# Two group-normed 5x5 convolutions: another buffer for one row tile, row additions earlier in the queue, a group mean later

## The chip, the cores and the metric

The kernel runs on one core of a Trainium2 chip. The metric is the device time of one execution in microseconds, taken as the median of several runs. The core has a matrix engine (TensorE, called PE in the profile, with its weight loads as PEld), a vector engine (VectorE, DVE), a scalar engine (ScalarE, ACT), a general engine (GpSimd, POOL) and a queue engine (SyncE, SP). Each engine works through its own list of instructions in the order in which the program gave them to it, and waits where an instruction needs something that is not ready. Transfers are issued here from SP's queue (image rows, statistics pieces, weights, results) and from POOL's queue (the copies and additions described below).

## The reference

There are eight images of 32 channels and 252 x 252 pixels in float32. Two layers follow each other, and each does the same thing with its own weights:

```
def layer(x, weight):
    g = groupnorm(x, 16 groups of 2 channels, eps 1e-5)   # mean and variance over 2*252*252 values
    return x + conv5x5(g, weight)                         # reflect-padded at the borders
x = layer(layer(x, L0_conv_weight), L1_conv_weight)
```

The reference computes the convolution by FFT; the kernel computes it directly. The normalisation is folded into the weights (a scale per channel) and a bias, and the residual addition of x is folded in as further weight entries.

## The kernel before, in words

**Tiling.** In the code the two layers are `l = 0` and `l = 1`, and below they are named by this index. An image is cut into 8 chunks of 16 row pairs (`c = 0..7`), so there are 8 x 2 x 8 = 128 units `(b, l, c)`. A unit is a Winograd-like convolution over rows: row differences and sums of the input are formed (points 0 to 5), multiplied on PE with transformed weights `u`, and combined into four output rows. PE works through the points in the order 2, 4, 1, 3 and later 0 and 5; each is three products (`product`, L671 to L682, `h = 0, 1, 2`), and each float32 product stands in the trace as two matmul records.

**Row differences v.** Points 4, 3, 1 and 0/5 need the tile `v`, the differences or sums of rows two apart. For `l = 0` DVE computes `v` (`row_pairs`, L556, the subtraction is L561). For `l = 1` transfers compute it (`row_sums`, L544): one call with `add = False` copies the unit's rows from `y` into `v` (POOL's queue, L551), and a later call with `add = True` adds the rows two further down onto it (L553, and L554 for the last two rows from the next chunk). The additions must wait until the copy has landed. The pool of `v` has one buffer per name: `row_pairs` uses the name `v`, and `row_sums` uses `va`, except for the last ten units, where it alternates between the two. The last reader of a `v` is `points05` (L603) on DVE. `point4` (L590, DVE) is the first to read the finished `v`.

**Order.** Nothing is scheduled by a compiler. Every piece of work is entered in a table with a due time (`at(t, fn, ...)`), the table is sorted by time, and the instructions are issued in that order. The times are not clock times: they only set the order on each engine. Units have slots starting at `begin(i)`, and the list `order` interleaves `l = 0` of image b+1 with `l = 1` of image b. Around the first image it runs

```
... (0,0,7) (1,0,0) (1,0,1) (0,1,0) (0,1,1) (1,0,2) (0,1,2) (1,0,3) ...
i:    7       8       9       10      11      12      13      14
```

so that (0,1,0) and (0,1,1) are the only two units with `l = 1` that follow directly on each other before the end of the list. With the times of the code, `begin(7)` is 107.1, `begin(8)` 122.4, `begin(9)` 132.6, `begin(10)` 147.9 and `begin(11)` 168.3.

**Statistics and weights.** When an image's last chunk of a layer is reached, `finish_stats` enters six steps: `moments` (DVE, L328 to L336), `group_mean` (PE, L342 and L344: tiny matmuls with averaging matrices into the spare columns of bank `m24[0]`), `deviations` (DVE, L351 to L357), `group_var` (PE, L363), `variance` (DVE L369 and ACT L371) and `inverse` (DVE, to L383). Then the weights are scaled by ACT for the points 2 and 4, then 1 and 3, then 0 and 5 (`scale_points`, L511), and POOL adds the residual's entries to each group (`add_residual`, L479, four instructions per group). PE's products of a point need its scaled weights with the residual added. I call the three groups of `add_residual` the first, second and third residuals.

**What stands near each other on POOL's list.** POOL has, besides `row_sums` and `add_residual`, the reflected borders of the input tiles `xs` (`borders`, L148 to L154), which wait for input loads issued by SP (L143).

Of the kernel before, what the change touches and what calls it, by code (L numbers as in the profile page):

```python
# [56 lines left out]
def tile_conv_preact_x2(ctx: ExitStack, tc: tile.TileContext, x: bass.AP, w0: bass.AP, w1: bass.AP, out: bass.AP):  # L57
    nc = tc.nc
    B, C, H, W = x.shape
# [5 lines left out]
    NCH = 8  # L65
# [26 lines left out]
    def at(t: float, fn, *args, **kw):  # L92
        table.append((t, len(table), fn, args, kw))
# [67 lines left out]
    def once(b: int, c: int) -> bool:  # L161

        return c < (NCH - 1, 3)[b] if b < 2 else False

    def parts(b: int, c: int):

        if once(b, c):
            return ((0, 10), (10, 6)) if (b, c) == (0, 0) else ((0, 2), (2, 14))
        return ((0, ROWS),) + (((ROWS, 2),) if c == NCH - 1 else ())
# [216 lines left out]
    def finish_stats(b: int, l: int, *times):  # L386
        for t, fn in zip(times, (moments, group_mean, deviations, group_var, variance, inverse)):
            at(t, fn, b, l)
# [86 lines left out]
    def add_residual(eng, u, ks):  # L475
        for cp, rp in quads:
            to = (2 * (1 - cp) + (1 - rp)) * Q
            dst = u[quad(cp, rp), ks, 1 + cp, to : to + Q]
            eng.tensor_add(dst, dst, resid[quad(cp, rp), ks])  # L479
# [53 lines left out]
    def transform(t0: float, t1: float, b: int, l: int, c: int, free: float = -100.0, now=(0, 0, 0)):  # L533
# [4 lines left out]
        def source():  # L538
            if l == 0:
                nxt = xs[b, c + 1] if c + 1 < NCH else xtail[b]  # L540
                return xs[b, c][:, :, 0:256:2], nxt[:, :, 0:256:2]
            return ytile[b, c], ytile[b, c + 1] if c + 1 < NCH else ytail[b]

        def row_sums(add: bool):  # L544

            t, nxt = source()
            if not add:
                i = max(order.index((b, l, c)) - order.index((B - 2, 1, NCH - 2)), 0)
                got["v"] = vpool.tile([P, ROWS, wi], F32, tag=("va", "v")[i % 2], name=f"v_{b}_{l}_{c}")
                got["vt"] = got["v"].rearrange("p (t i) w -> p t i w", i=4)  # L550
                G.dma_start(got["v"], t)  # L551
            else:
                G.dma_start(got["v"][:, 0 : ROWS - 2], t[:, 2:ROWS], accum_op=ALU.add)  # L553
                G.dma_start(got["v"][:, ROWS - 2 : ROWS], nxt[:, 0:2], accum_op=ALU.add)  # L554
# [70 lines left out]
        if (b, l, c) == order[0]:  # L625
            at(t0 - 33.3, row_quads, 0, 2)
            at(t0 - 31, point2, 0, 2)
            for fn in (row_pairs, point4):
                at(t0, fn, 0, 2)
            at(t0 + 0.2, row_quads, 2, 4)  # L630
            at(t0 + 0.2, row_pairs, 2, 4)
            at(t0 + 0.2, last_rows)
            at(t0 + 0.2, point2, 2, 4)
            at(t0 + 0.2, point4, 2, 4)
            at(t0 + 4.9, point1)
            at(t0 + 5.5, point3)
            at(t0 + 6.2, points05)
        else:
            if l:
                two = begin(order.index((b, l, c)) - 2)  # L640
                at(two + 1.45, row_sums, False)
                at(two + 11.0, row_sums, True)
            else:
                at(t0, row_pairs)
            for dt, fn in ((2, row_quads), (3.2, last_rows), (3.6, point2)):
                at(t0 + dt, fn)
            at(max(t0 + 4.2, free + 9.45) if l else t0 + 4.2, point4)
            at(max(t0 + 5.5, free + 7.8), point1)
            at(max(t0 + 5.6, free + (11.1 if by_columns(*now) else 10.25)), point3)
            at(t1, points05)  # L650
            if by_columns(b, l, c):
                at(t1 + 1.5, columns)
# [292 lines left out]
    order = [(0, 0, c) for c in range(NCH)]  # L945
# [4 lines left out]
    for n in ((0, 1, 0), (B - 2, 1, NCH - 2)):  # L950
        i = order.index(n)
# [8 lines left out]
    def by_columns(b: int, l: int, c: int) -> bool:  # L960
        if l == 0:
            return c < NCH - 1 and (b > 1 or (b == 1 and c > 1))
        return c in ((1, 3, 5) if b == B - 1 else ((1, 3) if b == B - 2 else (1, 3, 5)))
# [4 lines left out]
    def begin(i: int) -> float:  # L968

        return sum(10.2 + (own + [0.0])[j] + (late[j - 1] if j else 0.0) for j in range(i))  # L970


    t0 = -100.0
# [37 lines left out]
    at(t0 + 32.5, variance, 0, 0)  # L1011
    at(t0 + 33.5, inverse, 0, 0)
    transform(t0 + 64, 0.0, *order[0])
    at(t0 + 19, residual_blocks)
    at(t0 + 63.7, first_point, 2)
# [11 lines left out]
    for i, (b, l, c) in enumerate(order):  # L1027
        t0, t1, t2 = (begin(i + j) for j in range(3))
        if i in at_once:
            conv(b, l, c, t0, t1, m05=(extra[:, 0], extra[:, 1]))  # L1030
        elif i + 1 == len(order):

            conv(b, l, c, t0, t0 + 12.75, 0.0, 0, 2, m05=(extra[:, 0], extra[:, 1]))
            conv(b, l, c, t0 + 12.75, t0 + 20.4, 0.0, 2, 4, m05=(sums05[:, 0], sums05[:, 1]))
        elif i + 2 == len(order):
            conv(b, l, c, t0, t1, t1 + 10.3, later=5.1)
        else:
            conv(b, l, c, t0, t1, t2, later=10.2 + own[i + 1])
        if i + 1 < len(order):
            transform(t0 + (6.3 if i == 0 else 2.9), t1 + 0.2, *order[i + 1], free=t0, now=(b, l, c))  # L1040
            nb, nl, ncx = order[i + 1]
            k = inputs.index((nb, ncx)) + 2
            if nl == 0 and 2 < k < len(inputs):
                for part in parts(*inputs[k]):
                    early = once(*inputs[k]) or nb == 0
                    at(t0 + (14.0 if nb == 0 and part[0] == ROWS else 4.0 if early else 9.5), load, *inputs[k], *part)
                    at(t1 + (0.2 if early else 9.0), borders, *inputs[k], *part)
                    if once(*inputs[k]):
                        kb, kc = inputs[k]
                        t = 5.25 if part[0] == 0 and (kb, kc) != (1, 0) else 13.55 if kb else 8.5  # L1050
                        at(t1 + t, even_columns, *inputs[k], *part)
        if c == 0 and any(by_columns(b, l, k) for k in range(NCH)):
            t = begin(i - 1) if l == 0 and b > 1 else t2 if l == 0 else t0
            at(t + 5.4, halve_middle, b, l)
            at(t + 8.2, column_weights, b, l)
        if b and l == 0 and c == 0:
            at(t0 + 0.1, begin_sums, b, 1)

        if l == 0 and b + 1 < B:
            wide = 1 if b == 0 else 2  # L1060
            if c == 0:
                for j in range(2):
                    at(begin(i - 1) + 1.0 if b > 1 else t0 + (8.0 if b else 1.0), load_piece, b + 1, j)
            if c < NPIECE // 2:
                for j in range(2):
                    p = 2 * c + j
                    t = (t1 if wide == 2 and j else t0) + (8.6 + 2.5 * j if wide == 1 else 9.8)
                    if b == 1 and p < 4:
                        t = begin(NCH + (1, 1, 2, 2)[p]) + (9.8, 12.4, 9.8, 15.5)[p]
                    at(t, piece_sums, b + 1, p)  # L1070
                    if p + 2 < NPIECE:
                        at(t + 2.6, load_piece, b + 1, p + 2)
            if c == 2:
                at(t0 + 14, fetch_weights, b + 1, 0)
            if c == NCH - 1:
                finish_stats(b + 1, 0, *(t0 + t for t in (1.55, 3.5, 3.6, 6.9 if b else 7.7, 7.8, 8.4)))
                for j, ks in enumerate(pairs):
                    at(t0 + (9.5, 10.4, 11.3)[j], scale_points, b + 1, 0, ks)
                    at(t0 + (10.4, 12.3, 14)[j], lambda b=b, ks=ks: add_residual(G, scaled[b + 1, 0], ks))
        if l == 0 and c == NCH - 1:  # L1080
            te = t0 + 15.3
            at(te + 0.1, fetch_weights, b, 1)
            finish_stats(b, 1, *(te + t for t in (3.0 if b < B - 1 else 4.4, 6.85, 6.86, 10.25 if b else 9.9, 12.82, 13.55)))
            for j, ks in enumerate(pairs):
                at(te + (14.5, 15.5, 21)[j], scale_points, b, 1, ks)
                at(te + (15.5, 17.5, 22)[j], lambda b=b, ks=ks: add_residual(G, scaled[b, 1], ks))
# [36 lines left out]
```

## Time and profile before

| quantity | value |
|---|---|
| median of 3 runs | 1921.32 us (1920.58 to 1922.4) |
| the profiled execution's own time | 1922.81 us |
| its span, first to last instruction | 1921.0 us |
| PE busy | 1864.5 us, 97% of the span |
| PE weight loads (beside the matmuls) | 954.9 us |
| DVE busy | 1673.9 us |
| ACT busy | 1394.6 us |
| POOL busy | 385.1 us |
| mean granted PE clock | 0.990 |

Busy time is the time in which an engine executes something; the rest of the span is waiting. The list of groups gives for each kind of instruction its line, its engine, its tiles (written before, read after the arrow), its number, its busy time and its mean duration in ns, then the idle time directly before it and what ended that idle time. The list of waits sums these idle times per pair of waiter and releaser: total, number of times, longest. The timeline lists instructions by start time and length, neighbours of one kind merged (x12 means twelve records), with the idle time before them in brackets and the presumed releaser after the arrow. The stretch table gives, for a window, each engine's busy time and count, the granted PE clock as a share of full speed, the busy share of the 16 DMA engines and the bytes moved.

### The profile page before, as it was taken

What the parts mean: (1) busy time and instruction counts of PE and PEld (TensorE: products, weight loads), DVE (VectorE), ACT (ScalarE), POOL (GpSimd) and SP (SyncE); (2) the same over time, 40 slices, a digit from 0 to 9 for tenths busy, and PEclk for the clock granted to TensorE, in tenths of its full rate; (3) what the DMA queues carried; (4) which work ended last, traced back from release to release, by engine and by line L of the source; (5) the groups of instructions that cost most, each with busy time, mean ns of one, the idle gap of its engine ahead of it and who ended that gap; (6) DMA issues with size and microseconds to landing.
All of it is one profiled execution on the core that took longest, in us unless ns stands there. A gap on an engine that the chain in (4) does not pass through costs nothing.

```text
span 1921.0 us, 19939 instructions
## 1 busy us (share of the span) xinstructions
PE 1864.5 (97%) x5134; PEld 954.9 (50%) x5134; DVE 1673.9 (87%) x2923; ACT 1394.6 (73%) x2688; POOL 385.1 (20%) x733
## 2 busy tenths in 40 slices
PE   5998899999999999999999999999999999999998
PEld 4443355545555455544555445554455545544445
DVE  7987699989998899989999899997999989988675
ACT  5887577777787787777887777886787766665575
POOL 4542211131111211122111311113111131111210
PEclk8999899999999999999999999999999999999999
DMA  9877689989999899999999989998999978985695
GB/s 276 206 167 206 147 233 218 238 216 225 245 227 221 212 262 223 223 234 208 248 230 218 230 216 249 225 224 217 215 259 212 236 168 183 202 190 149 168 229 112
DMA packets 248626, 411.40 MB, mean 214 GB/s; under 512 B 19520, under 2 KB 215488, under 8 KB 238144
## 3 DMA queue, kind: packets, MB, share of 16 engines
q1 hardware_dynamic: 220384, 272.09, 60.4%
q0 software_dynamic: 27648, 135.28, 28.0%
q10 hardware_dynamic: 480, 2.77, 0.4%
q8 instruction: 40, 0.66, 0.1%
q14 instruction: 74, 0.61, 0.1%
HBM read 207.41 MB, written 67.39 MB: 143 GB/s over the span
## 4 chain that ended last, share of the span: by engine, by line
PE 83%; DMA 5%; ACT 4%; DVE 4%; issue 2%; POOL 1%; SPq 0%; ACTq 0%; DVEq 0%; POOLq 0%
PE pairs L679 30%; PE m L679 28%; PE sums L679 9%; PE extra L701 6%; PE sums L701 6%; PE extra L679 4%; DMA v<-y 2%; DMA st<-in_x_dram 2%; ACT o L916 1%; POOL u L479 1%; ACT junk L854 1%; ACT st L231 0%; ACT y L777 0%; ACT sd L731 0%; DVE sd L742 0%
## 5 line engine op out<-in xcount | busy, mean ns | idle before, releaser
L679 PE MATMUL m<-t,u 128*128 128x508 f32 (+3 forms) x1560 | 682.0, 585 | 21.4 <-POOL u L479 12.8
L679 PE MATMUL pairs<-t,u 128*128 128x504 f32 (+2 forms) x1548 | 688.8, 584 | 4.2 <-ACT pairs L723 2.8
L679 PEld LDWEIGHTS m<-t,u 128*128 128x128 f32 x1560 | 294.3, 190 | 346.4 <-issue 299.5
L679 PEld LDWEIGHTS pairs<-t,u 128*128 128x128 f32 x1548 | 290.0, 189 | 329.9 <-issue 303.5
L916 ACT COPY o<-y 64x508 f32<-64x508 f32 x496 | 326.8, 659 | 8.7
L679 PE MATMUL sums<-t,u 128*128 128x508 f32 (+5 forms) x492 | 208.4, 572 | 0.0
L725 ACT COPY pairs<-m 128x504 f32<-128x504 f32 (+1 forms) x129 | 72.5, 562 | 151.1 <-PE m L679 123.2
L742 DVE SCALAR_TENSOR_TENSOR sd<-sd,pairs 128x504 f32<-128x504 f32 (+2 forms) x258 | 164.2, 670 | 18.4 <-PE pairs L679 15.2
L854 ACT ACTIVATE junk<-y,negk 128x1008 bf16<-128x1008 f32 (+1 forms) x144 | 147.3, 1023 | 25.2 <-PE extra L701 14.9
L603 DVE SCALAR_TENSOR_TENSOR t<-v 128x1024 f32<-128x1024 f32 (+1 forms) x128 | 157.2, 1228 | 9.5 <-PE sums L679 9.5
L731 ACT COPY sd<-m 128x504 f32<-128x504 f32 (+2 forms) x258 | 137.2, 584 | 18.6 <-DVE sums L788 12.5
L590 DVE SCALAR_TENSOR_TENSOR t<-v 128x512 f32<-128x512 f32 (+2 forms) x129 | 90.4, 701 | 65.7 <-DMA v<-y 52.0
L701 PE MATMUL extra<-sdiff,wc 128*128 128x252 f32 (+2 forms) x560 | 141.6, 374 | 0.6 <-ACT extra L705 0.4
L701 PEld LDWEIGHTS extra<-sdiff,wc 128*128 128x128 f32 x560 | 104.2, 188 | 74.6 <-issue 51.4
L679 PEld LDWEIGHTS sums<-t,u 128*128 128x128 f32 x492 | 91.7, 188 | 94.6 <-issue 88.2
L767 ACT ACTIVATE y<-sums 128x508 f32<-128x508 f32 (+2 forms) x80 | 42.5, 580 | 130.3 <-PE sums L679 130.3
L148 POOL COPY xs<-xs 64x32 f32<-64x32 f32 (+3 forms) x74 | 35.2, 476 | 488.3 <-DMA xs<-in_x_dram 378.4
L561 DVE TENSOR_TENSOR v<-xs 128x1792 f32<-128x1792 f32 (+1 forms) x65 | 130.2, 2003 | 1.8 <-issue 0.5
L701 PE MATMUL sums<-d,u 128*128 128x252 f32 (+2 forms) x560 | 130.5, 375 | 0.0
L237 ACT ACTIVATE st<-st,negk 128x1134 f32<-128x1134 f32 x98 | 121.7, 1242 | 3.2
L553 POOL DMA_DIRECT2D v<-y x64 | 55.3, 863 | 319.2 <-DMA v<-y 319.2
L701 PEld LDWEIGHTS sums<-d,u 128*128 128x128 f32 x560 | 105.0, 189 | 26.2 <-issue 12.8
(171 smaller groups left out, 2467.7 us busy)
## 6 DMA issues: line engine op xcount, KB each, us to landing
xs<-in_x_dram SPq DMA_DIRECT2D x176, 504.0 KB, 11.6
v<-y POOLq DMA_DIRECT2D x64, 1032.0 KB, 5.4
st<-in_x_dram SPq DMA_DIRECT2D x111, 567.0 KB, 6.9
out_dram<-o SPq DMA_DIRECT2D x488, 126.0 KB, 5.3
v<-y POOLq DMA_DIRECT2D x64, 903.0 KB, 10.5
u<-ud SPq DMA_DIRECT2D x15, 1152.0 KB, 5.6
xs<-in_x_dram SPq DMA_DIRECT2D x30, 441.0 KB, 6.5
xs<-in_x_dram SPq DMA_DIRECT2D x28, 472.5 KB, 10.8
```

Source lines behind the costliest of these rows:

```text
L237: A.activation(junk, src, AF.Square, bias=negk, accum_out=acc[:, 1, i : i + 1])
L553: G.dma_start(got["v"][:, 0 : ROWS - 2], t[:, 2:ROWS], accum_op=ALU.add)
L561: V.tensor_sub(v[:, r0:r1], t[:, r0 + 2 : r1 + 2], t[:, r0:r1])
L590: stt(ts[b, l, c][0][:, 1, j0:j1], vt[:, :, 1], -2.0, vt[:, :, 2], ALU.mult, ALU.add)
L603: stt(t, got["vt"][:, :, 0:2], 4.0 if l else -4.0, got["vt"][:, :, 2:4], ALU.mult, ALU.add)
L679: T.matmul(dst, u[:, k, 2 - i, :], rhs[:, j0 + i0 : j0 + i1, i : i + wo], start=(i == 0 and not add), stop=(i == 2), skip_group_check=add,)
L701: T.matmul(dst[:, 0, use], w, rhs[:, use], start=(i == 2), stop=True, skip_group_check=(i != 2))
L725: A.copy(dst, src)
L731: A.copy(got["sd"][:, 1 + e], m24[e][:, 0:n])
L742: stt(d, d, -2.0, pairs13[e][:, 0:n], ALU.mult, ALU.add)
L854: A.activation(dst, src, AF.Square, bias=negk, scale=1.0 if i else -1.0, accum_out=acc[:, 1, at_ : at_ + 1])
L916: copy(got["o", h][halves[s], 0:m, cp::2], got["y"][halves[cp], r : r + m, :])
```

## The change

Three places change.

- In `row_sums`, unit (0,1,1) takes its `v` from the buffer name `v` instead of `va`. All other units keep their name.
- In `transform`, the additions to `v` of every unit with `l = 1` are entered at 8.4 instead of 11.0 after the start of the slot two before the unit. The copy stays at 1.45.
- In the main loop, the group mean of layer index 0 for images 1 to 7 is entered at 4.4 instead of 3.5 after the slot's start, and the step `deviations` behind it at 4.5 instead of 3.6. The other four steps keep their times.

```diff
             if not add:
-                i = max(order.index((b, l, c)) - order.index((B - 2, 1, NCH - 2)), 0)
+
+                i = max(order.index((b, l, c)) - order.index((B - 2, 1, NCH - 2)), 1 if (b, c) == (0, 1) else 0)
                 got["v"] = vpool.tile([P, ROWS, wi], F32, tag=("va", "v")[i % 2], name=f"v_{b}_{l}_{c}")
...
                 at(two + 1.45, row_sums, False)
-                at(two + 11.0, row_sums, True)
+                at(two + 8.4, row_sums, True)
...
             if c == NCH - 1:
-                finish_stats(b + 1, 0, *(t0 + t for t in (1.55, 3.5, 3.6, 6.9 if b else 7.7, 7.8, 8.4)))
+                finish_stats(b + 1, 0, *(t0 + t for t in (1.55, 4.4, 4.5, 6.9 if b else 7.7, 7.8, 8.4)))
```

## The prediction, written before the changed kernel was run

> **What bounds the kernel now.** I read the page first (busy times, then the chain that ended last), then PE's waits, then the timeline around each of PE's idle places.
>
> ```profile
> PE 1864.5 (97%) x5134; PEld 954.9 (50%) x5134; DVE 1673.9 (87%) x2923; ACT 1394.6 (73%) x2688; POOL 385.1 (20%) x733
> PE 83%; DMA 5%; ACT 4%; DVE 4%; issue 2%; POOL 1%; SPq 0%; ACTq 0%; DVEq 0%; POOLq 0%
> ```
>
> PE is busy 1864.5 of 1921.0 us and carries 83% of the last chain. The change removes no matmul, so it can only act on the 56.5 us in which PE stands still, and on its clock. PE's waits say where most of these are (waiter, releaser, total us, times, longest):
>
> ```profile
> PE m L998 <- DMA st<-in_x_dram: 14.6, 1, 14.6
> PE m L679 <- POOL u L479: 12.8, 1, 12.8
> PE m L342 <- DVE mv L332: 4.8, 6, 0.8
> PE m L679 <- ACT o L916: 2.9, 5, 0.8
> PE pairs L679 <- ACT pairs L723: 2.8, 7, 0.5
> ```
>
> The first is the program's start and is not touched. The single wait of 12.8 us and the three small ones, which come once per image, are what the three edits are near.
>
> **Edit 1, the other buffer for (0,1,1).** PE first, then POOL, then DVE around the hole:
>
> ```profile
> 181.36 4.60 PE L679 MATMUL sums<-t,u 128*128 128x378 f32 x12
> 198.81 8.39 PE L679 MATMUL m<-t,u 128*128 128x508 f32 x12 [12.85 <-POOL u L479]
> ...
> 176.77 1.21 POOL L554 DMA_DIRECT2D v<-y  x1
> 195.87 0.55 POOL L551 DMA_DIRECT2D v<-y  x1 [17.89 <-DVE t L603]
> 196.43 3.84 POOL L479 TENSOR_TENSOR u<-u,resid 32x64 f32<-32x64 f32 x8
> ...
> 190.73 0.70 DVE L590 SCALAR_TENSOR_TENSOR t<-v 128x516 f32<-128x516 f32 x1 [11.64 <-DMA v<-y]
> ```
>
> PE stops at 181.36 + 4.60 = 185.96 and wants the first products of (0,1,0). Their weights lack the residual, and the residuals (196.43) stand on POOL behind L551 (195.87), the copy for (0,1,1). That copy waits for L603 of (0,1,0), because both units use `va`. With the name `v` it waits for L603 of (1,0,1), which DVE ran at 172.54 for 1.22 us, so it is free when POOL is, at 177.98. ACT's first two scalings (L511) start at 177.26 and 179.54 and take 0.94 each, so two groups of residuals (3.84 us for 8) are done near 182.4. PE then goes on at 185.96 without waiting: 12.85 us gone.
>
> What is late next: point 2 needs no `v` and takes half of PE's usual 5.11 us pitch for 12 records, to 188.52. Point 4 needs L590, and L590 waits for the additions to (0,1,0)'s own `v`, issued at 176.19 and landed at 190.6. They stand ahead of the freed copy on the same queue and I leave their landing where it was. So PE stands from 188.52 to 190.73 + 0.70 + 0.1 = 191.5: a new gap of 3.0 us.
>
> The clock adds to both. The row of 198.81 takes 8.39 us for 12 records; the same 12 take 5.27 us at 222.55. So 3.1 us of the old hole's price is clock. The stretch table (PE busy, PEld, DVE, ACT, POOL, granted clock, DMA share, GB/s):
>
> ```profile
> 198.80:204.80 6.00, 5.99 (x7) 2.50 (x8) 0.00 (x0) 0.51 (x1) 4.78 (x13) 0.50 0.63 153
> 1771.50:1774.90 3.40, 1.32 (x4) 0.31 (x3) 3.40 (x6) 0.20 (x1) 0.37 (x1) 1.00 0.27 39
> 1774.90:1778.30 3.40, 3.40 (x6) 1.36 (x5) 2.67 (x10) 1.80 (x3) 0.90 (x3) 0.52 0.81 303
> ```
>
> A gap of only 2.08 us, at 1772.27, was followed by 3.4 us at clock 0.52: the next 8 records took 5.37 us, where 8 at the usual pitch take 0.17 + 8 x 0.425 = 3.57, a loss of 1.8 us. The Trainium skill, page "TensorE: Matmul & The Clock Gate", section "Part 1: The HAM clock gate (the "warmup" mystery)", has the clock halve after at least one idle window of about 3.4 us, windows running freely; by that a gap of 3.0 us, shorter than a window, should cost nothing more. The trace speaks against this: the window 1771.50 to 1774.90 held 1.32 us of matmul and was still followed by half speed. By the rule edit 1 gains 12.85 + 3.1 - 3.0 = 13.0 us; by the row it gains 1.8 less, **11.2 us**. I take the row, as it is the nearer gap.
>
> Other costs of edit 1: the additions for (0,1,1) now stand before the borders and the third residuals, and wait for the copy. The copy starts when the additions of (0,1,0) are through; with landings of 4.5 to 9.7 us from issue for the 64 copies it should land 3 to 7 us after 190.6. Then POOL needs 0.86 + 1.2 for the additions, 0.6 for borders and 1.5 to 1.9 for the third residuals: ready between 198 and 202. PE wants them for points 0 and 5 after four points at 5.11 us per two plus the 3.0 and 1.8: 185.96 + 10.2 + 4.8 = 201. Cost 0 to 1 us; I take 0. The next layer-0 unit's `row_pairs` (L561) writes the same buffer and needs L603 of (0,1,1), which is ahead of it on DVE anyway: nothing. DVE's tail of (1,0,1), from L742 at 191.35 to L758 at 196.9, was inside the hole and now runs beside PE's points 4 and 1; PE's third point needs L757 (ends 196.2) not before 198, so there is cover of 2 us.
>
> If the freed copy shares the engines with the additions instead of following them, they land up to one copy's time later, 4.5 us, and edit 1 gains 6.7. Range of edit 1: 6.7 to 13.0.
>
> **Edit 2, the additions at 8.4.** Per layer-1 unit two issues move (L553 0.86 us, L554 1.2 us), 64 times. In the ordinary slots POOL's list between 8.4 and 11.0 holds nothing else, since borders come 9.0 after the start of the following layer-0 slot and the copy at 1.45; the order stays and so does the time. SP's list is not touched. The order changes at (0,1,1) (ahead of borders, above), near the end (additions for (7,1,1) ahead of the third residuals: the copy issued at 1774.53 landed in 5.5 us, at 1780.0, and ACT frees these residuals only at 1783.8, so nothing), and for (b,1,0), b = 1 to 6, where the additions pass the first residuals. Image 1:
>
> ```profile
> 407.09 2.23 POOL L479 TENSOR_TENSOR u<-u,resid 32x64 f32<-32x64 f32 x4 [12.04 <-ACT u L511]
> 409.27 0.87 POOL L553 DMA_DIRECT2D v<-y  x1
> 421.40 0.70 DVE L590 SCALAR_TENSOR_TENSOR t<-v 128x516 f32<-128x516 f32 x1 [3.79 <-DMA v<-y]
> 433.80 5.31 PE L679 MATMUL m<-t,u 128*128 128x504 f32 x12 [0.83 <-ACT o L916]
> 439.50 1.96 PE L679 MATMUL pairs<-t,u 128*128 128x504 f32 x4 [0.39 <-ACT pairs L723]
> ```
>
> The copy (issued 394.25, 7.2 us) had landed at 401.4, but POOL sat 12.04 us in front of the residuals for ACT's scaling. The additions went out at 409.27 and 409.86 behind 2 MB of input loads (SP, from 401.81) and took over 11 us; DVE stood 3.79 us at L590. DVE then never idled until L586 at 432.96, whose end at 433.65 releases PE (the name ACT o is only the last event before). ACT waited 2.19 us for DVE at 429.35, then ran full until L723 at 438.78. Both small PE gaps thus hang on the 3.79 us.
>
> With edit 2 the additions go out near 401.5, at the same moment as the loads. The nearest row is the pair at 432.58 and 433.12 with input loads from 432.92 on: landed after 9.3 and 10.0 us. That gives about 412, before DVE arrives at 421.40 - 3.79 = 417.6. DVE then reaches L586 near 429.2, PE needs its result at 432.97; ACT's chain moves up by its 2.19 us, L723 ends near 437.3, PE wants it 5.1 us after 432.97, at 438.1. Both gaps close. The residuals are no later: POOL is done with the additions at 403.4 and ACT frees them at 407.0. Summed over images 1 to 6 the timeline has before L586's product 0.83, 0.26, 0.68, 0.48, 0.50, 0.84 = 3.6 us and before the pairs 0.39 + 4 x 0.40 = 2.0: **5.6 us**, range 2.5 (ACT's chain keeps the second gap and takes part of the first) to 5.6.
>
> **Edit 3, the group mean at 4.4.** PE and DVE in image 2's statistics:
>
> ```profile
> 377.87 0.35 PE L342 MATMUL m<-mv,avg_ss 128*128 128x1 f32 x2 [0.79 <-DVE mv L332]
> 377.56 0.17 DVE L332 TENSOR_SCALAR mv<-tot 128x2 f32<-128x2 f32 x1
> ```
>
> Products are entered at 0.85 steps, so 3.5 lies between the second and third product of point 4 and 4.4 behind the third. PE reached L342 at 377.08, after the edit 0.85 us later at 377.93; the mean is out at 377.73 and released PE at 377.87. The six waits of 0.8 us vanish: **4.8 us**. DVE's own wait for the mean (0.38 us at 378.55) grows by some 0.06, and between 3.6 and 4.5 DVE's list holds nothing else, so only the next transform's steps behind it move by that. PE's variance matmul comes at 381.0 and its input at 379.4: 1.6 us of cover. If another 0.1 us of lateness on DVE occurs, 0.1 per image comes back. Range 3.5 to 4.9. For image 1, at 147.76, PE did not wait and gains nothing.
>
> **Sum.** 11.2 + 5.6 + 4.8 = 21.6 us. The profiled execution took 1922.81 (its span and 1.81 us around it) and would take 1901.2. It stood 1.5 above the median of the runs, 1921.32; from that I predict **1899.7 us**.
>
> **Rivals.**
>
> *No half clock after the new gap* (chance 0.15): gain 13.0 + 5.6 + 4.8 = 23.4, 1897.9 us. For it: the rule, and windows that run freely, so their phase may spare the gap. Against: the row at 1774.90.
>
> *The buffer edit pays, the small gaps come back* (0.14): DVE and ACT are so full at the image changes (DVE without idle from 421.40 to past 441) that PE's 1.6 us saved per image is waited for a few products later. Gain 11.2 plus up to 4, 1906 to 1910. Against it: between these places PE runs hundreds of us without a gap.
>
> *Edit 1 doesn't free the residuals* (0.05), as something else still holds L551: gain 10.4, 1910.9.
>
> *Slower: additions push the input loads at the image changes* (0.05). Both go out near 401.5. If the loads give way, `xs` lands later than 414.99, POOL's borders (417.11, 1.0 us) follow, and DVE's L561, which moves up to 425.4, waits. It starts to cost when the loads are over 9.4 us late; to eat all 21.6 us they must be 13 us late in each of six images (6 x 3.6). Two more us each gives 1934. Against: the fastest pair of additions lands in 6.4 us, so they can hold the loads up by about that.
>
> The forecast has 0.61. About 0.2% (3.8 us) is what a measurement of this kernel tells from no change. A gain below that needs two edits to fail and the third to cost: 0.03 for within, 0.05 for slower, 0.92 for faster. The range, 1896.5 to 1907.5, takes the ends 13.0, 5.6 and 4.9 with 1 us for measurement below, and the shared-engine end of edit 1 with part of the small gaps lost above.
>
> **What would show it.** Right: PE's list of waits has no 12.8 us on L479; instead a wait near 3 us at the second point of (0,1,0), released by DVE L590, then some 3.4 us at half clock; L551 right after L554 at 178; no L342 waits on L332; L553 ahead of L479 near 400 with DVE's 3.8 us waits gone and six pairs of small gaps gone. Wrong: L551 still at 195; L590 later than 191; new PE waits on L586 or L723 after each image change; borders waiting for `xs` followed by DVE waits at L561.

## The result, and the profile after

| kernel | median, us | runs | lowest to highest | ratio to before, 95% interval |
|---|---|---|---|---|
| before, timed beside it | 1921.53 | 4 | 1920.58 to 1922.40 | |
| after | 1895.71 | 4 | 1895.29 to 1895.99 | 0.9866 (0.9848 to 0.9883) |

The change is faster by 25.8 us; the forecast was 21.6 us (1899.7), and the result lies 0.8 us below the low end of the range, 1896.5. The profiled execution took 1895.29 us with a span of 1893.5, against 1922.81 and 1921.0 before.

The page after, engine totals and the chain that ended last:

```profile
PE 1858.3 (98%) x5134; PEld 955.4 (50%) x5134; DVE 1673.8 (88%) x2923; ACT 1396.8 (74%) x2688; POOL 381.7 (20%) x733
PE 93%; DMA 3%; DVE 1%; ACT 1%; POOL 1%; issue 0%; SPq 0%; ACTq 0%; DVEq 0%; POOLq 0%
```

TensorE runs the same 5134 matmuls. It stands still for 1893.5 - 1858.3 = 35.2 us instead of 56.5, and carries 93% of the chain instead of 83%. It is also busy 6.2 us less for the same work. Of that, 1.3 us lie at the hole and 1.4 us at the last image, where less runs at half clock, and busy time at half clock counts double. Another 3.4 us lie at the six image changes, where no half clock was; what they are stands under edit 2 below. The waits of PE (waiter, releaser, total us, times, longest; from line 546 on the numbers are one higher than before):

```profile
PE m L999 <- DMA st<-in_x_dram: 14.6, 1, 14.6
PE m L680 <- DVE t L591: 2.5, 2, 1.9
PE m L680 <- DVE var L369: 2.1, 1, 2.1
PE pairs L680 <- ACT pairs L724: 1.2, 2, 0.7
```

The 12.8 us on L479 and the 4.8 us of six waits on L332 are gone. L723 (now L724) has 1.2 us left of 2.8. A new line has come: 1.9 us on L591, the stop that the prediction put at 3.0 us. Its place, in the timeline of PE, POOL and DVE:

```profile
186.18 2.72 PE L680 MATMUL m<-t,u 128*128 128x508 f32 x6
190.84 4.49 PE L680 MATMUL m<-t,u 128*128 128x508 f32 x6 [1.95 <-DVE t L591]
195.16 5.27 PE L680 MATMUL pairs<-t,u 128*128 128x508 f32 x12
...
176.54 1.21 POOL L555 DMA_DIRECT2D v<-y  x1
177.08 1.22 POOL L552 DMA_DIRECT2D v<-y  x1
178.65 1.79 POOL L479 TENSOR_TENSOR u<-u,resid 32x64 f32<-32x64 f32 x4 [0.35 <-ACT u L511]
...
190.00 0.70 DVE L591 SCALAR_TENSOR_TENSOR t<-v 128x516 f32<-128x516 f32 x1 [10.48 <-DMA v<-y]
```

Read it from POOL: the copy for unit (0,1,1) (L552) now goes out at 177.08, right behind the additions for (0,1,0), where it stood until 195.87 before. The residuals (L479) follow at 178.65, and PE enters point 2 of (0,1,0) at 186.18 without a wait. Point 4 lacks L591, which lacks the additions, landed 188.05 and 189.87. Its first six records take 4.49 us where six take 2.72 one row up: half clock again, and the table of stretches shows how long (PE busy, PEld, DVE, ACT, POOL, granted clock, DMA share, GB/s):

```profile
188.22:191.64 3.42, 1.47 (x4) 0.49 (x3) 1.64 (x3) 3.29 (x14) 0.00 (x0) 1.00 1.04 400
191.64:195.05 3.41, 3.41 (x5) 1.35 (x4) 3.41 (x8) 0.69 (x3) 1.13 (x2) 0.50 0.64 254
1744.70:1748.11 3.41, 1.45 (x4) 0.38 (x2) 3.41 (x7) 0.00 (x0) 0.00 (x0) 1.00 0.58 102
1748.11:1751.52 3.41, 3.29 (x8) 1.43 (x8) 3.24 (x12) 1.34 (x3) 0.67 (x2) 1.00 0.62 228
```

The second row is one stretch of 3.41 us at 0.50. The last two rows are the old 2.08 us stop at the last image (var L369): before, 3.4 us at 0.52 followed it; now no half clock does.

For the other two edits the lines after are these, three from image 1's change and one from the group mean of image 2:

```profile
388.45 0.86 POOL L554 DMA_DIRECT2D v<-y  x1 [4.74 <-DMA v<-y]
394.41 4.94 POOL L479 TENSOR_TENSOR u<-u,resid 32x64 f32<-32x64 f32 x8 [3.99 <-ACT u L511]
404.65 0.69 DVE L591 SCALAR_TENSOR_TENSOR t<-v 128x516 f32<-128x516 f32 x1
366.04 0.35 PE L342 MATMUL m<-mv,avg_ss 128*128 128x1 f32 x2
```

The additions (L554) now stand ahead of the residuals (L479), DVE enters L591 without the 3.79 us of before, and PE enters the group mean without its 0.79 us. Where the time went is read best by laying PE's records of the two profiles side by side, one by one, and following how the start of the same record shifts:

| place | predicted gain, us | gain in the two profiles, us |
|---|---|---|
| start of the program, to 180 us | 0 | -0.4 |
| edit 1, the hole at 186 us and what follows | 11.2 | 12.2 |
| edit 2, six image changes | 5.6 | 1.78 + 1.21 + 1.62 + 1.42 + 1.44 + 1.78 = 9.3 |
| edit 3, six group means | 4.8 | 0.80 + 0.85 + 0.84 + 0.86 + 0.83 + 0.83 = 5.0 |
| the last image's stop: no half clock behind it | 0 | 1.4 |
| sum | 21.6 | 27.5 |

27.5 us is the difference of the two spans. It is 1.7 more than that of the medians, because the profile of before was one of the longer executions (1922.81 against 1921.53) and that of after one of the shorter ones (1895.29 against 1895.71).

### The profile page after: what moved, and what is told of

Read it like the earlier page. It is cut to its first block, busy times and chain, and to the rows that moved or that the text cites. A ratio compares the mean times of both kernels' runs of the same rounds, so it can differ in the third digit from the quotient of the medians.

```text
span 1893.5 us, 19933 instructions
## 1 busy us (share of the span) xinstructions
PE 1858.3 (98%) x5134; PEld 955.4 (50%) x5134; DVE 1673.8 (88%) x2923; ACT 1396.8 (74%) x2688; POOL 381.7 (20%) x733
## 4 chain that ended last, share of the span: by engine, by line
PE 93%; DMA 3%; DVE 1%; ACT 1%; POOL 1%; issue 0%; SPq 0%; ACTq 0%; DVEq 0%; POOLq 0%
PE m L680 33%; PE pairs L680 33%; PE sums L680 10%; PE sums L702 6%; PE extra L702 6%; PE extra L680 4%; DMA st<-in_x_dram 1%; DMA v<-y 1%; POOL u L479 0%; DMA xs<-in_x_dram 0%; ACT o L917 0%; DMA wraw<-in_L_conv_weight_dram 0%; SPq L143 0%; PE m L342 0%; DVE bn L276 0%
## 5 line engine op out<-in xcount | busy, mean ns | idle before, releaser
L591 DVE SCALAR_TENSOR_TENSOR t<-v 128x512 f32<-128x512 f32 (+2 forms) x129 | 90.3, 700 | 56.5 <-DMA v<-y 39.2
L562 DVE TENSOR_TENSOR v<-xs 128x1792 f32<-128x1792 f32 (+1 forms) x65 | 130.1, 2001 | 1.8 <-DMA st<-in_x_dram 0.5
L554 POOL DMA_DIRECT2D v<-y x64 | 55.3, 864 | 373.5 <-DMA v<-y 373.5
```

Of the source, the lines that this page charges most:

```text
L562: V.tensor_sub(v[:, r0:r1], t[:, r0 + 2 : r1 + 2], t[:, r0:r1])
L591: stt(ts[b, l, c][0][:, 1, j0:j1], vt[:, :, 1], -2.0, vt[:, :, 2], ALU.mult, ALU.add)
```

## Experiments

Each kernel was timed beside the kernel before, whose median was 1921.47 beside e1 to e4, 1921.69 beside e5 to e7, 1921.62 beside e8 to e10 and 1921.93 beside e11 and e12. Theory to be tested: the three edits act in three different places and add up, each by taking away a stop of PE. Rivals: one edit carries the others, or the stops come back elsewhere.

**One edit at a time.** First the buffer alone:

```diff
-                i = max(order.index((b, l, c)) - order.index((B - 2, 1, NCH - 2)), 0)
+                i = max(order.index((b, l, c)) - order.index((B - 2, 1, NCH - 2)), 1 if (b, c) == (0, 1) else 0)
```

> Edit 1 alone (the other buffer for (0,1,1); additions stay at 11.0, group mean at 3.5). Theory 'each edit removes its own stops of PE': the shift of PE's starts between the two profiles at (0,1,0) is 12.2 us, so about 1909.3 us, with a PE gap of 2 us in front of point 4 and one stretch of 3.4 us at half clock behind it. Rival 'the edits help each other, alone they have the sizes of the prediction': 11.2 us, about 1910.3; and if the additions at 8.4 are needed to get them ahead of the third residuals, less.

Measured 1911.38 (1910.75 to 1911.89), ratio 0.9947 (0.993 to 0.9964): 10.1 us. PE's waits, and two rows of the stretch table around the stop:

```profile
PE m L342 <- DVE mv L332: 4.8, 6, 0.8
PE m L679 <- DVE t L590: 4.0, 2, 3.4
187.33:190.75 3.42, 1.80 (x5) 0.50 (x3) 0.00 (x0) 3.31 (x12) 0.00 (x0) 1.00 1.04 307
190.75:194.16 3.41, 1.59 (x4) 0.86 (x5) 2.44 (x6) 1.92 (x5) 0.00 (x0) 1.00 0.99 357
```

The hole is gone, the six L342 waits stand as before. The additions landed later than in the changed kernel (at 191.6 instead of 189.9), so the stop is 3.44 us and not 1.95; and yet no half clock follows. The longer stop was the one without it. The 10.1 us are less than either figure expected. Side by side with before, this profile gains 12.0 us at the hole, as the changed kernel does, and loses 1.0 elsewhere, 0.6 of it before 180 us; the rest is that the profile of before was one of the longer executions.

Then the additions alone:

```diff
-                at(two + 11.0, row_sums, True)
+                at(two + 8.4, row_sums, True)
```

> Edit 2 alone (additions at 8.4; same buffer, group mean at 3.5). Theory 'own stops': the starts shift by 1.7, 1.1, 1.5, 1.3, 1.4 and 1.6 us in the six image changes, together 8.6 us, so about 1912.9 us, and the hole of 12.8 us at 186 us stays. Rival 'sizes of the prediction': 5.6 us, about 1915.9, the other 3 us come only together with the other edits.

Measured 1911.64 (1910.13 to 1912.48), ratio 0.9949 (0.9934 to 0.9963): 9.8 us, where the prediction had 5.6. PE's waits:

```profile
PE m L679 <- POOL u L479: 12.7, 1, 12.7
PE m L342 <- DVE mv L332: 4.9, 6, 0.8
PE pairs L679 <- ACT pairs L723: 0.8, 2, 0.5
```

The hole and the L342 waits stay, of the seven stops on L723 five are gone, and so are the six before L586's product. Side by side with before, PE's starts gain 1.78, 1.21, 1.62, 1.43, 1.44 and 1.78 us at the six image changes, 9.3 in all, the same as in the changed kernel.

Then the group mean alone:

```diff
-                finish_stats(b + 1, 0, *(t0 + t for t in (1.55, 3.5, 3.6, 6.9 if b else 7.7, 7.8, 8.4)))
+                finish_stats(b + 1, 0, *(t0 + t for t in (1.55, 4.4, 4.5, 6.9 if b else 7.7, 7.8, 8.4)))
```

> Edit 3 alone (group mean at 4.4). Theory 'own stops': 0.9 us at each of six images, 5.5 us together, about 1916.0 us. Rival 'sizes of the prediction': the waits as the list shows them, 4.8 us, about 1916.7. A third possibility: PE's arrival 0.9 us earlier is waited for at L587/L724 after the image change while the additions are still late, then nearly nothing, 1920 to 1921.

Measured 1915.91 (1914.68 to 1917.05), ratio 0.9972 (0.9961 to 0.9983): 5.6 us. The L342 waits are gone and PE's starts gain 0.83 to 0.86 us at each; the hole and the stops at the image changes are still there. The three together give 10.1 + 9.8 + 5.6 = 25.5 us against 25.8 for the whole change. Each of the three gains is known to some 2 to 3 us only, but place by place the profiles say the same: each edit takes away its own stops, and none comes back for want of the others.

**The group mean the other way.** The changed kernel with the mean one step earlier than it ever was:

```diff
-                finish_stats(b + 1, 0, *(t0 + t for t in (1.55, 4.4, 4.5, 6.9 if b else 7.7, 7.8, 8.4)))
+                finish_stats(b + 1, 0, *(t0 + t for t in (1.55, 2.7, 2.8, 6.9 if b else 7.7, 7.8, 8.4)))
```

> The changed kernel with the group mean one product earlier than before the change (2.7, deviations 2.8). If a stop of PE costs its whole length from start to start and nothing gives it back, each of six images has a wait 0.85 us longer than before's 0.9: 6 x 1.75 = 10.5 us over the changed kernel, about 1906 us, and L342's waits show 1.6 us each. Rival 'PE has slack after the image change that takes part of it back': under 1903. Rival 'longer stops also halve the clock': each stop of 1.8 us could bring a stretch at half clock, up to 1.7 us more each, to 1916.

Measured 1909.48 (1907.40 to 1910.90): 13.8 us over the changed kernel's 1895.71. Waits and timeline:

```profile
PE m L342 <- DVE mv L332: 9.8, 6, 1.7
368.15 0.35 PE L342 MATMUL m<-mv,avg_ss 128*128 128x1 f32 x2 [1.65 <-DVE mv L332]
366.29 0.70 DVE L758 TENSOR_TENSOR sums<-pairs,sd 128x508 f32<-128x508 f32 x1 [1.18 <-ACT y L780]
367.83 0.17 DVE L332 TENSOR_SCALAR mv<-tot 128x2 f32<-128x2 f32 x1
```

One product (0.85 us) earlier makes each wait 0.85 us longer, 0.79 to 1.65, so the place in PE's list is what edit 3 acts on. Starts are 1.64 to 1.69 us later per image, at one image 3.39, where a stretch of half clock (at 1286.6) came behind the wait: 11.7 us together. Another 2.4 us came at the stop at 188.6 us, which has two such stretches behind it here. So a wait of 1.65 us cost 1.7, or 3.4 with half clock.

**Can the last image's stop be taken away?** In the changed kernel PE waits 2.08 us for the variance (L369). It was entered later, behind the product that had to wait for it:

```diff
-            finish_stats(b, 1, *(te + t for t in (3.0 if b < B - 1 else 4.4, 6.85, 6.86, 10.25 if b else 9.9, 12.82, 13.55)))
+            finish_stats(b, 1, *(te + t for t in (3.0 if b < B - 1 else 4.4, 6.85, 6.86, 10.25 if b else 9.9, *((12.82, 13.55) if b < B - 1 else (13.9, 14.2)))))
```

> The changed kernel, and for the last image the variance step on DVE entered behind PE's third product of point 2 of (6,1,7), at 13.9 instead of 12.82 (inverse at 14.2). Theory 'PE waits there because the product writes the bank that L369 has still to read': the stop of 2.08 us goes, with what each stop costs beyond its listed length some 2.3 us, so about 1893.4 us, and up to 1.7 less in executions where the clock halved there. Rival 'the next thing is as late': L369 and the scaling of the last weights come 1.3 us later, POOL's residuals with them; if PE needs them before, the stop comes back in front of (7,1,0), about 1895.7.

Measured 1896.87 (1896.12 to 1898.63), no gain: 1.2 us over the changed kernel. PE, and ACT at the same time:

```profile
1753.44 5.38 PE L680 MATMUL pairs<-t,u 128*128 128x508 f32 x12 [2.71 <-ACT pairs L724]
1751.91 0.94 ACT L511 ACTIVATE u<-u,rstd 128x768 f32<-128x768 f32 x1 [1.00 <-DVE rstd L383]
1752.75 0.64 ACT L724 ACTIVATE pairs<-m,means 128x508 f32<-128x508 f32 x1
```

The stop moved one point on. The pairs' seed (L724) stands on ACT behind the first scaling of the image's weights (L511), which waits for the inverse deviation. So the next kernel puts that scaling behind the seed:

```diff
-                at(te + (14.5, 15.5, 21)[j], scale_points, b, 1, ks)
+                at(te + (14.5 if b < B - 1 else 14.9, 15.5, 21)[j], scale_points, b, 1, ks)
```

> The changed kernel, with the variance of the last image at 13.9 and the inverse at 14.2 as in e5, and the first scaling of that image's attention weights at 14.9 instead of 14.5, so that ACT reaches the seed of the pairs first. If the stop of e5 (2.71 us on ACT's pairs seed) stood only because that scaling was ahead of the seed on ACT, the stop is gone: 2.08 us listed in the changed kernel, some 2.3 from start to start, about 1893.4 us. If ACT is full here, the stop comes back behind the next ACT instruction that TensorE needs, and the time stays at about 1895.7. A half-clock window behind a stop is worth another 1.6 us either way.

Measured 1893.75 (1892.65 to 1895.67), 2.0 us under the changed kernel, though the two ranges overlap.

```profile
1752.05 5.52 PE L680 MATMUL pairs<-t,u 128*128 128x508 f32 x12 [0.79 <-ACT pairs L724]
1751.36 0.64 ACT L724 ACTIVATE pairs<-m,means 128x508 f32<-128x508 f32 x1
```

Of e5's stop of 2.71 us, 0.79 is left: the order on ACT was the cause of the rest. Side by side with the changed kernel, the starts gain 1.5 us here.

**Why do the additions at 177 us take 13 us?** Those for (0,1,0) are issued at 175.97 and 176.54, behind four input loads of unit (1,3) on SP's queue, the last of them at 170.47, 2 MB together. Here the loads go to POOL's queue, behind the additions:

```diff
-    def load(b: int, c: int, lo: int, n: int):
+    def load(b: int, c: int, lo: int, n: int, eng=S):
...
-                    at(t0 + (14.0 if nb == 0 and part[0] == ROWS else 4.0 if early else 9.5), load, *inputs[k], *part)
-                    at(t1 + (0.2 if early else 9.0), borders, *inputs[k], *part)
+                    pool = inputs[k] == (1, 3)
+                    at(t0 + (14.0 if nb == 0 and part[0] == ROWS else 4.0 if early else 18.0 if pool else 9.5), load, *inputs[k], *part, G if pool else S)
+                    at(t1 + (0.2 if early else 12.0 if pool else 9.0), borders, *inputs[k], *part)
```

> The changed kernel, and the four input loads of (1,3), 2 MB, issued from POOL's queue behind the first two residuals instead of from SP's queue at 167 us; its borders behind the third residuals. Theory 'the additions to (0,1,0)'s v are late because the input loads hold the engines': they land after 6.5 to 7.5 us instead of 13.3, before 184 us; DVE's L591 no longer waits 10 us, PE's stop of 2 us at point 4 goes and with it the half clock: 2.2 to 3.9 us, 1891.8 to 1893.5 us. Rival 'the landing is set by something else' (the landing of the first copy, other traffic): additions land near 190 again, no change. Second rival 'POOL is too late': four issues of about 1 us before the next additions delay the third residuals, a new stop at point 0 of (0,1,0), 1896 or more.

Measured 1897.43 (1896.75 to 1898.61), 1.7 us over the changed kernel. The additions did land in 6.50 and 6.65 us, at 180.8 and 181.5, and the stop on L591 went. But the loads now stood ahead of the next additions, those of (0,1,1):

```profile
184.48 0.97 POOL L554 DMA_DIRECT2D v<-y  x1
185.10 1.26 POOL L555 DMA_DIRECT2D v<-y  x1
206.59 0.70 DVE L591 SCALAR_TENSOR_TENSOR t<-v 128x516 f32<-128x516 f32 x1 [8.46 <-issue]
214.74 5.37 PE L680 MATMUL pairs<-t,u 128*128 128x508 f32 x8 [1.93 <-ACT pairs L724]
```

These took 20.4 and 21.4 us; L591 follows right on their landing (206.51), and with DVE late, ACT's seed and PE's products came late. This row too has half clock: 8 records in 5.37 us. The two changes e5 and e6 in one kernel:

> Both of the two edits before together. If the stops are independent: 1895.7 less 2.3 less 2.2 to 3.9, so 1889.5 to 1891.2 us.

Measured 1899.52 (1897.48 to 1900.12): the stops of both were in it, that at 213 us with 3.06 us instead of 1.93. Then the loads one step later, behind the additions of both units:

```diff
-  ... else 4.0 if early else 18.0 if pool else 9.5), load, ...
+  ... else 4.0 if early else 18.8 if pool else 9.5), load, ...
```

> The changed kernel, with the four loads of unit (1,3) issued by POOL at 18.8, behind the residual additions of both unit (0,1,0) and unit (0,1,1). If the additions took 13.3 us only because 2 MB of loads stood ahead of them, both sets now land within some 6.5 to 8 us, the stop on DVE's t (1.95 us) and the half clock behind it are gone, and what is left is a stop of about 1 us at the pairs seed: about 1893 to 1894.5. The second stop of e6 (1.93 us at 212.8) goes too. If instead what counts is that POOL's queue is longer, the copy of v for unit (0,1,2) is late and the time is above 1896.

Measured 1894.19 (1892.21 to 1896.12), 1.5 us under the changed kernel, but with runs on both sides of it. Side by side, its profile gains 2.6 us at this stop. The additions of (0,1,0) land in 6.5 and 6.7 us, those of (0,1,1) in 9.0 and 10.5, and PE waits for neither. Then e8 and e9 together:

> e8 and e9 in one kernel: the two stand 1550 us apart and share no instruction, so the gains add: about 1891 to 1892.5. If either returns its stop elsewhere, as e5 and e6 did, the time is at or above that of the better one.

Measured 1891.20 (1890.81 to 1892.80), ratio 0.9836 (0.9816 to 0.9855). POOL's order and the two stops that are left:

```profile
186.67 0.88 POOL L554 DMA_DIRECT2D v<-y  x1 [4.54 <-DMA v<-y]
187.81 3.34 POOL L143 DMA_DIRECT2D xs<-in_x_dram  x4
192.24 5.35 PE L680 MATMUL pairs<-t,u 128*128 128x508 f32 x12 [1.04 <-ACT pairs L724]
1747.71 5.52 PE L680 MATMUL pairs<-t,u 128*128 128x508 f32 x12 [0.79 <-ACT pairs L724]
```

Between 40 us and the last matmul no stretch at half clock is left.

**The changed kernel and the better one again, side by side.**

> The changed kernel itself, beside e12 on one chip: about 1895.7 us. Its second profile has the same instructions, so what differs from the first is the chip's own: if the half clock depends on how a stop falls in a window that runs on its own, the stop on DVE's t (1.95 us) and the one at the last image (2.08 us) stay within some tenths of a microsecond of their length, or move with the landing of the additions, while the half-clock window behind them may be absent at one and present at the other. If the half clock followed from the length of the stop, the same pattern returns: behind the 1.95 us one, not behind the 2.08 us one.

> The kernel of e10 again, beside the changed one: about 1891.2 us, so 4 to 5 us under e11, with no half-clock window behind 190 us and none at the tail, where the stops that are left have 1.04 and 0.79 us.

The changed kernel has 1895.20 (1894.80 to 1896.45), the better one 1891.02 (1890.48 to 1891.33): 4.2 us apart, and the two ranges don't touch. That is the 1.5 and 2.6 us of the two places together. The better version beats before by 1.6% (ratio 0.9838, 0.9823 to 0.9852). The second profile of the changed kernel, PE at the stop and the stretches at both stops:

```profile
191.80 4.49 PE L680 MATMUL m<-t,u 128*128 128x508 f32 x6 [2.61 <-DVE t L591]
189.08:192.50 3.42, 0.81 (x3) 0.49 (x3) 1.54 (x3) 3.06 (x11) 0.00 (x0) 1.00 1.05 406
192.50:195.91 3.41, 3.41 (x5) 1.35 (x4) 3.41 (x8) 0.50 (x1) 1.32 (x2) 0.50 0.58 233
1745.56:1748.97 3.41, 1.83 (x5) 0.53 (x3) 3.25 (x5) 0.00 (x0) 0.00 (x0) 1.00 0.60 107
```

The same kernel has a stop of 2.61 us here and 1.95 there, as the additions landed at 190.84 and at 189.87. The pattern of half clock came out as in the first profile (behind the first stop, not behind the one at the last image), so this run didn't tell luck from length; what tells is the table in the last section.

## Why the prediction fell short

**Edit 1: right, within the scatter of one landing.** The path was as told: copy at 177, residuals in time, point 2 without a wait, a stop at point 4 behind L591, half clock for one stretch. Predicted were a stop of 3.0 us and 1.8 us of half clock; the two profiles of the changed kernel have 1.95 and 2.61 us, the first with a loss of 4.49 - 2.72 = 1.77 us; e1 had 3.44 us and no loss. The first profile gains 12.2 us, 1.0 more than predicted; 0.7 of that is L591, which started at 190.00 rather than at the 190.73 that the prediction left in place. The second is 0.66 us behind it at this stop, so 11.6. The rule that was weighed there, no half clock behind so short a gap, would have had 13.0.

**Edit 2: the mechanism right, the term mis-sized, 5.6 for 9.3 us.** This is the step that failed: "Summed over images 1 to 6 the timeline has before L586's product" 3.6 us "and before the pairs" 2.0. It took the idle time in brackets for the price of a stop, 0.83 + 0.39 for image 1. The rows around these two, one of before and three of after:

```profile
431.30 1.67 PE L701 MATMUL sums<-d,u 128*128 128x189 f32 x8
...
418.62 1.67 PE L702 MATMUL sums<-d,u 128*128 128x189 f32 x8
420.13 5.23 PE L680 MATMUL m<-t,u 128*128 128x504 f32 x12
425.20 3.54 PE L680 MATMUL pairs<-t,u 128*128 128x504 f32 x8
```

Before, the product behind the columns started at 433.80, so 2.50 us after 431.30; now 420.13 - 418.62 = 1.51. That stop cost 0.99 us, not 0.83. The next one: 439.50 - 433.80 = 5.70 us before, 425.20 - 420.13 = 5.07 now: 0.63, not 0.39. Two things are missing in the bracket. Products overlap: a record lasts 0.58 us and the next one starts 0.42 after it, so the idle time counts from an end that lies 0.16 us behind the point at which the next start was due. And the second record behind a stop comes 0.50 or 0.53 us after the first, not 0.42, another 0.07 or 0.11 us. (The second stop's 0.63 is 0.39 + 0.16 and the first stop's 0.07, in rounded numbers; its own slow record comes on top.) So a listed 0.83 cost 1.06 and a listed 0.39 cost 0.67. Over the changes that is 6 x 0.24 + 5 x 0.28 = 2.8 us; 0.3 more came from a sixth stop before the pairs, listed with 0.02 us, and 0.6 from pauses at the column products (L701), 0.03 to 0.05 us each and 0.42 at the last change, of which the waits show nothing. 5.6 + 2.8 + 0.3 + 0.6 = 9.3. That all of it is edit 2's own is shown by e2.

**Edit 3: right,** 4.8 for 5.0 us; e3 and e4 showed that the place in PE's list is the cause. Here the bracket was nearly the price: the record behind these short products comes 0.51 us after the one before it with or without a stop.

**The last image: 1.4 us that the sum didn't have.** The prediction's own stretch table showed half speed behind the 2.08 us stop of before, but the sum left it as it was, as no edit is near. It doesn't belong to the stop: it came in the profiles of before, e1 and e6, and not in those of e2, e3, e4, e9 and the two of after, all with the same stop. It is in the difference of the profiles, and only by chance in that of the medians: without it the steps give 27.5 - 1.4 = 26.1 us, the medians 25.8.

**The rivals.** That the small gaps come back was refuted at every image change. No half clock behind the new stop: refuted for the changed kernel in both profiles, true for e1. Additions that push the input loads at the image changes: the push is there, the last load at image 1 took 15.5 us instead of 11.7, but it is far from the 9.4 us at which the prediction saw a cost, and DVE's L562 waits no more than before. In e6 the parts are exchanged: loads that push additions, at a cost. The range failed at its low end, because its end for edit 2, 5.6, was the sum of the brackets itself, taken as the most that could be won. (The ends 13.0, 5.6 and 4.9 with 1 us for measurement make 1896.8 and not 1896.5; the result lies below both.)

## What to carry to other kernels

Price a stop by the distance from start to start against the same distance where nothing waits, not by the idle time listed: with records that overlap, each stop between products cost 0.2 to 0.3 us more, which for stops of 0.4 us is more than half again. When a stop is taken away, look at what stands ahead of the next thing needed on its own engine's list (e5 and e8: one scaling ahead of a seed on ACT made 1.9 us of a stop of 2.7). Put small transfers that are needed soon ahead of large ones that are needed late, and for every reader at once: here, moving the loads behind one pair of additions and ahead of another lost time, behind both it gained.

## What the runs showed of the hardware

**Half clock follows a stretch that was too empty, not a long stop.** The granted clock changes at the ends of stretches of 3.41 us, and these run on whatever the program does: in the profile of before, the two changes to half clock at 191.25 and 1775.03 us lie 464 times 3.4133 us apart. Their phase can be read off each profile, and PE's busy time laid over them; a choice of stops from all profiles, each in a stretch at full clock:

| PE busy, share of the emptiest stretch | stop, us | kernel, place | half clock behind it |
|---|---|---|---|
| 0.03 | 3.58 | e8, 189 us | yes |
| 0.24 | 2.61 | after, second profile, 189 us | yes |
| 0.39 | 2.08 | before, last image | yes |
| 0.42 | 2.08 | after, last image | no |
| 0.43 | 1.95 | after, 189 us | yes |
| 0.43 | 1.93 | e6, 213 us | yes |
| 0.45 | 3.06 | e7, 213 us | no |
| 0.47 | 3.44 | e1, 189 us, over two stretches | no |
| 0.52 | 1.65 | e4, 365 us | no |
| 0.52 | 1.65 | e4, 1284 us | yes |
| 0.54 | 2.08 | after, second profile, last image | no |

Up to 0.39 it always followed, and from 0.45 on it didn't but for one row of e4. So a stop of 3.44 us was free of it and one of 1.95 was not: where a stop of 2 to 3.5 us falls in its stretch decides over another 1.4 to 1.8 us, and no stretch had to be idle as a whole. Why 0.42 and 0.43, and the two stretches of e4 at 0.52, went as they did stays open.

**What is issued ahead of a transfer decides when it lands.** 1 MB of additions took 13.3 us behind 2 MB of loads of another queue, and 6.5 us where the loads were issued only after it had landed (e6, e9). The loads did not go first as a whole: in the profile of after, the last of them, issued 5.5 us before the additions, landed 2.5 us after them, at 192.39, while the DMA engines were busy throughout (share 1.00 to 1.18 from 176 to 188 us). So the two queues shared the engines. On one queue, where only the order was changed, POOL's additions for (0,1,1) took 20.4 and 21.4 us behind the loads (e6) and 9.0 and 10.5 ahead of them (e9). Behind the loads on the other queue the landing also scattered, 13.3, 13.7 and 14.9 us in the two profiles of after and that of e8, whose instructions are the same there; with it the stop on L591 went from 1.95 over 2.61 to 3.58 us.
